# A projection's biases added in place in PSUM by VectorE, in place of bf16 products on TensorE

## The chip, the cores and the metric

The kernel runs on one core of one Trainium2 chip. The metric is the device time of one execution in microseconds (us); the span of the profile is the time from the first to the last instruction of the profiled execution. A core has five engines with a queue each, worked off in order: TensorE (PE; its weight loads are shown as PEld), VectorE (DVE), ScalarE (ACT), GpSimd (POOL) and SyncE (SP), which issues nearly all DMAs here. Engines wait for one another through semaphores. TensorE writes its results into PSUM, and VectorE and ScalarE read them there.

## The reference, cut to what matters

There are 128 graphs of 128 nodes with 64 features, and a dense matrix `adj` for each graph. The first layer is an edge network of 192 hidden units, the second one product with `adj` and a 64x64 matrix.

```python
h = jnp.maximum(_layernorm(x), 0.0)
mask = (adj > 0.0)
xj_proj = h @ W1a                               # W1a, W1b: halves of W1, 64x192 each
diff = h[:, :, None, :] - h[:, None, :, :]
e = relu(xj_proj[:, :, None, :] + diff @ W1b + b1)
hm = einsum('bjkh,bjk->bjh', e, mask)           # sum over the neighbours k of j
x = x + hm @ W2 + deg[..., None] * b2
h = jnp.maximum(_layernorm(x), 0.0)
x = x + einsum('bnm,bmf->bnf', adj, h) @ W.T
```

The sum inside relu splits into one term of node j, `h_j @ (W1a + W1b) + b1`, and one of node k, `-h_k @ W1b`. Both are projections of the nodes, made once for a graph. The biases in question are `b1` in the term of node j, and a bias of 64 columns beside it, made from `b1`, `W2` and `b2`, which is later multiplied by the degree.

## The kernel before

**Staging.** The graphs are worked in 32 groups of 4. A group has 24 jobs. A job fills a tile `g` of PSUM (two banks; a pool of three such tiles) by products on PE that select the projected rows of up to 12 neighbours ("slots") of each of 64 nodes, and then drains it. Jobs of kind 0 are drained by DVE (`hm<-g`, one reduction of 128x768), jobs of kind 1 by ACT (`T<-g`), and POOL adds up their slots (`T<-T`). The table `ORDER` has four jobs of kind 0, two of kind 1, and so on. I number the jobs of a group from 0 to 23; jobs 4, 5, 10, 11, 16, 17, 22 and 23 are of kind 1.

**What is woven in.** After each job's fill the tables `AHEAD`, `OWN` and `BEHIND` call pieces of work for the next group, this one, and the one before. Those around the change are, in order of jobs:

- after job 7: `pre_proj(g, 0)` of the next group, the projection of graphs 0 and 2 of that group;
- after job 8: `post0` (`py` on PE, then `ys<-py` on ACT); after job 10: `post1` (`pty` on PE reads `ys`; then `x1` and its norm on DVE);
- after job 9: `pre_edge_a` (`et<-iov` on ACT); after job 12: `pre_proj(g, 1)`, for graphs 1 and 3, and then `pre_stack`;
- after jobs 14 and 15: `edge_x` (`px` on PE, `X<-px` on ACT); after job 15: `post2` (four `h<-x` on ACT, tile `h2`); after job 16: `post3` (`pga` on PE reads `h2`).

**The projection.** `pre_proj` takes one of the three tiles of the pool of `g`, as `pp`: two banks, one for each graph of the pair. For each graph one fp32 product fills 448 columns: 192 of node k, 192 of node j, and 64 of the second layer's share. A second, bf16, product of a matrix of ones (`oneb`) and `biasp` adds the biases to columns 192 to 447. `biasp` holds them as three bf16 parts in three rows, made at the start in `weights_c` with the help of `id64`. Then ACT copies the first 384 columns to bf16 (`ca<-pp`), and makes `z<-pp` (four instructions) and `e<-pp` (two) from `pp`; DVE subtracts (`rest<-pp,ca`); ACT rounds the rest (`ca<-rest`), and POOL makes the third bf16 part (`ca<-rest,ca`). `pre_stack` copies the three parts by 12 DMAs on SP's queue into `k3` (`k<-ca` in the profile), from which the next group's jobs 0 and 1 read first. Ahead of them stand 12 DMAs `S<-S` on the same queue.

**What sets the order.** The products keep the order of the program on PE. On the other engines the order is fixed in the program only for the first group; after that, in each queue, a scheduler places the instructions when the kernel is built. It also chooses which of the three tiles of PSUM each `g` and `pp` takes. All engines' instructions go through one helper, so most of them carry the line of that helper (L198; L181 and L184 for products and transposes); the groups of the profile are told apart by their tiles.

Of the kernel before, what the change touches and what calls it, by code (L numbers as in the profile page):

```python
# [8 lines left out]
F32 = mybir.dt.float32  # L9
BF16 = mybir.dt.bfloat16  # L10
I32 = mybir.dt.int32
AF = mybir.ActivationFunctionType
ALU = mybir.AluOpType
# [137 lines left out]
def kernel(  # L151
# [28 lines left out]
    def mm(*args, **kw):  # L180
        return tc.keep_in_program_order(nc.tensor.matmul(*args, **kw))  # L181
# [21 lines left out]
    vec, act, pool, sp = (Engine(e) for e in (nc.vector, nc.scalar, nc.gpsimd, nc.sync))  # L203

    B, N, F = x.shape
    H = W1.shape[1]
    O = W2.shape[1]
    P = 128
# [19 lines left out]
    with ExitStack() as main:  # L228
        const = main.enter_context(tc.tile_pool(name="const", bufs=1))
        loads = main.enter_context(tc.tile_pool(name="loads", bufs=2))  # L230
        grp = main.enter_context(tc.tile_pool(name="grp", bufs=2))
        one = main.enter_context(tc.tile_pool(name="one", bufs=1))
# [4 lines left out]
        def gtile(name):  # L237
            return ps_g.tile([P, 2, 512], F32, tag="g", name=name)
# [14 lines left out]
        ident = const.tile([P, P], F32, tag="ident", name="ident")  # L253
        make_identity(nc, ident)

        id64 = const.tile([P, 4], F32, tag="id64", name="id64")
        vec.tensor_tensor(id64, ident[:, 0:4], ident[:, F : F + 4], ALU.add)
        ones = const.tile([P, P], F32, tag="ones", name="ones")
        pool.memset(ones, 1.0)
        oneb = const.tile([P, P], BF16, tag="oneb", name="oneb")  # L260
# [11 lines left out]
        for q in range(Q):  # L272
            s = slice(q * QN, (q + 1) * QN)
# [43 lines left out]
        bias = const.tile([P, H + O], F32, tag="bias", name="bias")  # L317
        wp = const.tile([P, 2 * H + O], F32, tag="wp", name="wp")
        wab = wp[:, H : 2 * H]
        biasp = const.tile([P, H + O], BF16, tag="biasp", name="biasp")  # L320

        def weight_loads():
            act.dma_start(w2a, W2[0:C0, :])
# [22 lines left out]
        def weights_b():  # L346
            pb = mtile("pb")
            mm(pb[:, 0:O], b1x, w2h, start=True, stop=True)
            vec.tensor_tensor(wab, w1[:, 0], w1[:, 1], ALU.add)
            pw = mtile("pw")  # L350
            tp(pw[:, 0:P], wab[:, 0:C0], ident)
            vec.tensor_tensor(bias[:, H : H + O], pb[:, 0:O], b2s, ALU.add)
            vec.tensor_scalar(wp[:, 0:H], w1[:, 1], -1.0, None, ALU.mult)
            vec.tensor_copy(wT, pw[:, 0:P])
            pc = mtile("pc")
            mm(pc[:, 0:O], wT, w2h, start=True, stop=True)
            return pc

        def weights_c(pc):
            left = bias  # L360
            for i in range(3):
                pt = one.tile([P, H + O], BF16, tag=f"bp{i}", name=f"bp{i}")
                vec.tensor_copy(pt, left)

                if i == 0:
                    vec.tensor_scalar(biasp, pt, id64[:, i : i + 1], None, ALU.mult)
                    vec.tensor_copy(wp[:, 2 * H : 2 * H + O], pc[:, 0:O])
                else:
                    vec.scalar_tensor_tensor(
                        biasp, pt, id64[:, i : i + 1], biasp, ALU.mult, ALU.add  # L370
                    )
                if i < 2:
                    nxt = one.tile([P, H + O], F32, tag=f"br{i}", name=f"br{i}")
                    vec.tensor_tensor(nxt, left, pt, ALU.subtract)
                    left = nxt

        def weights_d():
            pl = mtile("pl")
# [5 lines left out]
        def bc(t, n, axis):  # L384
            shape = list(t.shape)
            shape.insert(axis, n)
            return t.unsqueeze(axis).to_broadcast(shape)
# [150 lines left out]
        def pre_proj(g, r):  # L538

            d = groups[g]  # L540
            if r == 0:

                d["ca"] = grp.tile([P, 3, 2, G, H], BF16, tag="ca", name=f"ca{g}")

                d["z"] = grp.tile([P, G, H], F32, tag="z", name=f"z{g}")
                d["e"] = grp.tile([P, G, O], F32, tag="e", name=f"e{g}", bufs=3)
            pp = gtile(f"pp{g}_{r}")
            for p in range(2):
                s = slice(p * F, (p + 1) * F)
                mm(  # L550
                    pp[:, p, 0 : 2 * H + O], d["hT"][s, r], wp[s, :],
                    start=True, stop=False, skip_group_check=True,
                )
            for p in range(2):
                s = slice(p * F, (p + 1) * F)
                mm(
                    pp[:, p, H : 2 * H + O], oneb[s, :], biasp[s, :],
                    start=False, stop=True, skip_group_check=True,
                )
            x = pp[:, :, 0 : 2 * H].rearrange("n p (t u) -> n p t u", t=2)  # L560
            parts = [
                d["ca"][:, i].rearrange("n t (p r) u -> n r p t u", p=2)[:, r] for i in range(3)
            ]
            act.activation(parts[0], x, AF.Copy)
            rest = tmp.tile([P, 2, 2, H], F32, tag="rest", name=f"rest{g}_{r}")

            def zs():
                for p in range(2):
                    b = 2 * p + r
                    for us, f in ((slice(0, C0), AF.Abs), (slice(C0, H), AF.Relu)):  # L570
                        act.activation(
                            d["z"][:, b, us], x[:, p, 1, us], f, scale=d["ns"][:, b : b + 1]
                        )


            def es():
                for p in range(2):
                    b = 2 * p + r
                    act.activation(
                        d["e"][:, b], pp[:, p, 2 * H : 2 * H + O], AF.Copy,  # L580
                        scale=d["dn"][:, 0, b : b + 1],
                    )

            def second():
                act.activation(parts[1], rest, AF.Copy)

            def third(engine):
                for t in range(2):
                    engine.tensor_tensor(
                        parts[2][:, :, t], rest[:, :, t], parts[1][:, :, t], ALU.subtract  # L590
                    )

            def add_x():
                pool.tensor_tensor(d["e"], d["e"], d["x"], ALU.add)

            if g == 0:
                vec.tensor_tensor(rest, x, parts[0], ALU.subtract)
                return zs, es, second, third, add_x
            zs()
            es()  # L600
            vec.tensor_tensor(rest, x, parts[0], ALU.subtract)
            second()
            third(pool)
            if r == 1:
                add_x()
# [205 lines left out]
        class Job:  # L811
# [76 lines left out]
            5: (pre_count,),  # L888
            6: (lambda g: pre_slots(g, 4, D),),
            7: (lambda g: pre_proj(g, 0),),  # L890
            9: (pre_edge_a,),
            12: (lambda g: pre_proj(g, 1), pre_stack,),
            19: (pre_edge_b,),
            20: (pre_place,),
# [51 lines left out]
        pc = weights_b()  # L946
        load(1)
        weight_loads2()
        pre_hT(0)
        first_ranks(0, 0)  # L950
        weights_c(pc)
        constants()
        pre_rank(0)
        pre_count(0)
        steps = [pre_proj(0, 0), pre_proj(0, 1)]
        for (zs, es, second, third, add_x), engine in zip(steps, (pool, vec)):
            if engine is vec:
# [69 lines left out]
```

## Time and profile before

| | |
|---|---|
| time, median of 3 runs (lowest to highest) | 1011.81 us (1011.59 to 1017.17) |
| span of the profiled execution | 1013.2 us, 1.4 us above the median |
| PE, PEld busy | 963.8 us (95%), 721.6 us (71%) |
| DVE, ACT, POOL busy | 799.7 us (79%), 704.1 us (69%), 765.9 us (76%) |
| fp32 products `pp<-wp,hT` | 256 rows, 68.7 us busy |
| `hm<-g` on DVE | 512, 472.1 us busy, 948 ns each |
| HBM | 13.01 MB read, 4.19 MB written, 17 GB/s over the span |

The profile was taken of one execution; its page gives the span and no other time of that execution, and the single stages below are read from it. In its rows, out<-in names the tiles, and the number after a group is the busy time; "idle before" is the time that the engine stood still ahead of it, with what released it. Products overlap on PE and their ends are modelled, so a busy share of 95% doesn't say that PE has no time to spare. HBM's traffic is small against the time; the DMAs that matter are those between tiles of SBUF.

### The profile page before, as it was taken

The page shows a single profiled execution, that of the slowest core. Times are in us where ns is not written, and L with a number is a line of the kernel's source. Part 1 is how long each engine was busy: PE and PEld are TensorE (multiplying, and loading weights), DVE is VectorE, ACT ScalarE, POOL GpSimd, SP SyncE. Part 2 cuts the span into 40 slices and gives each one's busy share as a digit, 9 for nine tenths or more (in the row PEclk, how much of TensorE's full clock was granted, in tenths as well). Part 3 has the DMA queues.
Part 4 walks back from the last instruction along what each step waited for, and adds up shares of the span by engine and source line. Part 5 has one row for each costly group of instructions (what it writes and reads, how often), then busy time and mean ns, then how long its engine had stood idle before and what let it go on. Part 6 is the DMA issues. An engine that isn't in the chain of part 4 may idle for free.

```text
span 1013.2 us, 27270 instructions
## 1 busy us (share of the span) xinstructions
PE 963.8 (95%) x10314; PEld 721.6 (71%) x10314; DVE 799.7 (79%) x1769; ACT 704.1 (69%) x1732; POOL 765.9 (76%) x1134
## 2 busy tenths in 40 slices
PE   3899999999999999999999999999999999999996
PEld 2577777777777777777777777777767777777774
DVE  7767888777888877788877788877787877788863
ACT  5557876677777667777667787667786667787652
POOL 3278777787877777877778877777877778877783
PEclk9599999999999999999999999999999999999998
DMA  3526655556755556766555766545765555765420
GB/s 83 133 68 162 147 135 130 123 124 154 161 136 134 122 120 140 163 136 138 126 123 129 162 144 136 131 112 128 162 140 133 127 120 132 162 147 119 110 67 14
DMA packets 88296, 129.94 MB, mean 128 GB/s; under 512 B 47200, under 2 KB 63968, under 8 KB 88160
## 3 DMA queue, kind: packets, MB, share of 16 engines
q1 hardware_dynamic: 87584, 127.98, 55.2%
q8 instruction: 83, 1.36, 0.5%
q14 instruction: 53, 0.43, 0.1%
q10 hardware_dynamic: 576, 0.16, 0.1%
HBM read 13.01 MB, written 4.19 MB: 17 GB/s over the span
## 4 chain that ended last, share of the span: by engine, by line
PE 45%; DVE 25%; ACT 14%; DMA 5%; POOL 4%; issue 3%; SPq 2%; DVEq 1%; POOLq 0%; ACTq 0%
PE g L181 24%; DVE hm L198 9%; PE pe L181 8%; DVE S L198 8%; DMA k<-ca 4%; ACT ca L198 3%; PE px L181 3%; DVE u L198 3%; ACT et L198 3%; POOL T L198 3%; SPq L198 2%; PE pp L181 2%; PE py L181 2%; ACT h L198 2%; ACT T L198 2%
## 5 line engine op out<-in xcount | busy, mean ns | idle before, releaser
L198 POOL TENSOR_TENSOR T<-T 128x192 f32<-128x192 f32 (+2 forms) x768 | 543.6, 714 | 139.0 <-ACT T L198 99.1
L181 PEld LDWEIGHTS <-k 96*128 96x128 bf16 (+1 forms) x6144 | 412.4, 104 | 208.5 <-issue 87.4
L198 DVE TENSOR_REDUCE hm<-g 128x64 f32<-128x768 f32 x512 | 472.1, 948 | 110.4 <-PE g L181 108.6
L181 PE MATMUL g<-S,k 96*128 96x384 bf16 (+1 forms) x2048 | 392.1, 333 | 29.2 <-DMA k<-ca 14.3
L181 PE MATMUL g<-id,k 96*128 96x192 bf16 (+1 forms) x4096 | 384.1, 248 | 0.0
L198 ACT ACTIVATE T<-g 128x768 f32<-128x768 f32 x256 | 209.8, 821 | 48.5 <-PE g L181 48.5
L198 POOL TENSOR_TENSOR ca<-rest,ca 128x384 bf16<-128x384 f32 x126 | 114.0, 924 | 82.3 <-ACT ca L198 72.0
L198 ACT ACTIVATE ca<-pp 128x768 bf16<-128x768 f32 x64 | 51.3, 802 | 63.9 <-PE pp L181 63.9
L198 DVE TENSOR_TENSOR S<-qs,rks 128x1024 bf16<-128x1024 bf16 x93 | 86.9, 962 | 0.1
L198 ACT ACTIVATE hT<-ph 128x256 f32<-128x256 f32 x32 | 12.3, 383 | 104.0 <-PE ph L184 104.0
L181 PE MATMUL pe<-RT,X 128*64 128x128 f32 (+1 forms) x512 | 74.9, 285 | 0.0
L181 PE MATMUL pe<-mident,z 128*64 128x128 f32 (+1 forms) x512 | 68.8, 274 | 0.0
L181 PE MATMUL pp<-wp,hT 64*128 64x448 f32 x256 | 68.7, 614 | 0.0
L198 ACT ACTIVATE z<-pp,ns 128x128 f32<-128x128 f32 (+1 forms) x256 | 65.7, 347 | 0.0
L198 ACT ACTIVATE ca<-rest 128x768 bf16<-128x768 f32 x64 | 55.2, 863 | 11.6 <-DVE rest L198 11.6
L198 DVE TENSOR_TENSOR rest<-pp,ca 128x768 f32<-128x768 f32 x64 | 60.7, 948 | 3.2 <-ACT ca L198 3.1
L198 DVE TENSOR_SCALAR maskT<-adjT 128x512 bf16<-128x512 f32 x32 | 17.2, 538 | 52.7 <-PE pe L181 52.7
L198 ACT ACTIVATE et<-et,half 128x128 f32<-128x128 f32 x128 | 56.8, 449 | 0.0
L181 PEld LDWEIGHTS pe<-mident,z 128*64 128x64 f32 (+1 forms) x512 | 53.8, 164 | 0.0
L181 PEld LDWEIGHTS pe<-RT,X 128*64 128x64 f32 (+1 forms) x512 | 52.8, 164 | 0.1
L181 PE MATMUL px<-ca,S 128*128 128x192 bf16 x384 | 52.7, 246 | 0.0
L181 PE MATMUL px<-ca,R 128*128 128x192 bf16 x384 | 52.6, 246 | 0.0
(128 smaller groups left out, 1263.1 us busy)
## 6 DMA issues: line engine op xcount, KB each, us to landing
S<-S SPq DMA_DIRECT2D x372, 192.0 KB, 4.0
k<-ca SPq DMA_DIRECT2D x384, 96.0 KB, 2.2
adj<-in_adj_dram SPq DMA_DIRECT2D x32, 256.0 KB, 3.0
x<-in_x_dram SPq DMA_DIRECT2D x32, 128.0 KB, 2.7
out_dram<-ot SPq DMA_DIRECT2D x32, 128.0 KB, 2.2
w<-in_L_gnn_W_dram SPq DMA_DIRECT2D x2, 96.0 KB, 5.1
bias<-in_L_gnn_b_dram ACTq DMA_DIRECT2D x1, 96.0 KB, 4.6
w2a<-in_L_gnn_W_dram ACTq DMA_DIRECT2D x1, 32.0 KB, 2.2
```

Source lines behind the costliest of these rows:

```text
L181: return tc.keep_in_program_order(nc.tensor.matmul(*args, **kw))
L198: ins = f(*args, **kw)
```

## The change

The two bf16 products of each `pre_proj` are taken out. In their place one VectorE operation adds the biases to both graphs' columns 192 to 447 in place in PSUM. It reads `pp` (128 partitions, 2 x 256 fp32) and the fp32 tile `bias`, repeated for the two graphs. The ACT copies and everything else that reads `pp` now come after that operation. `weights_c` keeps one copy of what it did, since the bf16 parts of the biases are not needed, and `id64` goes.

```diff
-        id64 = const.tile([P, 4], F32, tag="id64", name="id64")
-        vec.tensor_tensor(id64, ident[:, 0:4], ident[:, F : F + 4], ALU.add)
...
-        biasp = const.tile([P, H + O], BF16, tag="biasp", name="biasp")
...
         def weights_c(pc):
-            left = bias
-            for i in range(3):
-                pt = one.tile([P, H + O], BF16, tag=f"bp{i}", name=f"bp{i}")
-                vec.tensor_copy(pt, left)
-
-                if i == 0:
-                    vec.tensor_scalar(biasp, pt, id64[:, i : i + 1], None, ALU.mult)
-                    vec.tensor_copy(wp[:, 2 * H : 2 * H + O], pc[:, 0:O])
-                else:
-                    vec.scalar_tensor_tensor(
-                        biasp, pt, id64[:, i : i + 1], biasp, ALU.mult, ALU.add
-                    )
-                if i < 2:
-                    nxt = one.tile([P, H + O], F32, tag=f"br{i}", name=f"br{i}")
-                    vec.tensor_tensor(nxt, left, pt, ALU.subtract)
-                    left = nxt
+            vec.tensor_copy(wp[:, 2 * H : 2 * H + O], pc[:, 0:O])
...
                 mm(
                     pp[:, p, 0 : 2 * H + O], d["hT"][s, r], wp[s, :],
-                    start=True, stop=False, skip_group_check=True,
-                )
-            for p in range(2):
-                s = slice(p * F, (p + 1) * F)
-                mm(
-                    pp[:, p, H : 2 * H + O], oneb[s, :], biasp[s, :],
-                    start=False, stop=True, skip_group_check=True,
-                )
+                    start=True, stop=True, skip_group_check=True,
+                )
+            biased = pp[:, :, H : 2 * H + O]
+            vec.tensor_tensor(biased, biased, bc(bias, 2, 1), ALU.add)
```

## The prediction

> **What bounds the kernel now.** I began with the page, its busy shares and the chain that ended last.
>
> ```profile
> PE 963.8 (95%) x10314; PEld 721.6 (71%) x10314; DVE 799.7 (79%) x1769; ACT 704.1 (69%) x1732; POOL 765.9 (76%) x1134
> PE 45%; DVE 25%; ACT 14%; DMA 5%; POOL 4%; issue 3%; SPq 2%; DVEq 1%; POOLq 0%; ACTq 0%
> ```
>
> PE leads both lines, but the chain changes engines: no engine alone is the end. So I took the sums of the waits, and then one group from the middle of the timeline.
>
> ```profile
> DVE hm L198 <- PE g L181: 108.6, 113, 2.5
> ACT ca L198 <- PE pp L181: 63.9, 34, 3.5
> PE g L181 <- DMA k<-ca: 14.3, 17, 7.2
> PE g L181 <- DVE hm L198: 12.7, 31, 0.5
> ```
>
> Once in nearly every group ACT stands ready for `ca<-pp` before PE has made `pp` (63.9 us in 34 waits), and PE's next job waits a little for a reduction (31 times 0.4 us).
>
> ```profile
> 466.23 1.02 PE L181 MATMUL pp<-wp,hT 64*128 64x448 f32 x4
> ...
> 466.73 0.94 DVE L198 TENSOR_REDUCE hm<-g 128x64 f32<-128x768 f32 x1
> ...
> 467.08 0.28 PE L181 MATMUL pp<-biasp,oneb 64*128 64x256 bf16 x2
> 467.40 0.81 ACT L198 ACTIVATE ca<-pp 128x768 bf16<-128x768 f32 x1 [1.87 <-PE pp L181]
> 467.73 0.48 PE L181 MATMUL g<-S,k 96*128 96x384 bf16 x2 [0.37 <-DVE hm L198]
> 467.80 1.81 DVE L198 TENSOR_REDUCE hm<-g 128x64 f32<-128x768 f32 x2
> 469.00 0.55 ACT L198 ACTIVATE e<-pp,dn 128x64 f32<-128x64 f32 x2
> 469.79 0.38 ACT L198 ACTIVATE ys<-py 128x256 f32<-128x256 f32 x1 [0.25 <-PE py L181]
> 471.15 0.44 PE L184 MATMUL pty<-ident,ys 128*128 128x128 f32 x2
> 473.91 0.28 PE L181 MATMUL pp<-biasp,oneb 64*128 64x256 bf16 x2
> 474.17 0.48 PE L181 MATMUL g<-S,k 96*128 96x384 bf16 x2
> 474.37 0.79 ACT L198 ACTIVATE ca<-pp 128x768 bf16<-128x768 f32 x1
> 477.42 0.81 ACT L198 ACTIVATE h<-x,mrb,rsb 128x64 f32<-128x64 f32 x2
> 478.89 0.61 PE L181 MATMUL pga<-adjT,h 128*64 128x128 f32 x8
> ```
>
> A row holds start, duration, engine and tiles; the bracket is the idle time before it. The next group's `pp` starts at 496.27, so a group takes 30.04 us. After the first `ca<-pp` (467.40) ACT goes from row to row almost without a gap until R at 481.98: in the 15.6 us to 483.0 it is idle for 0.9. PE gets to `pga` at 478.89, and the last of the four `h` that it reads ended at 477.42 + 0.81 = 478.23. ACT is thus only about 0.7 us ahead of PE there. A second limit stands at the end of the group, on SP's queue: 12 DMAs `S<-S` from 466.76, 12 `k<-ca` behind them from 476.79, and the jobs of the next group just catch the last ones.
>
> ```profile
> 485.62 0.33 PE L181 MATMUL g<-S,k 96*128 96x384 bf16 x1
> 486.12 0.32 PE L181 MATMUL g<-S,k 96*128 96x384 bf16 x1 [0.17 <-DMA k<-ca]
> ```
>
> Two such products elsewhere follow each other by 0.16 us, here by 0.50, and in job 1 0.15 more is lost: 0.5 us in a group.
>
> **The change part by part.** *Removed from PE:* a pair of bias products in each of 64 calls. The pair costs 474.17 - 473.91 = 0.26 us of PE's time; 64 x 0.26 = 16.6 us if nothing else stood in the way. At r = 0 job 8 starts at 467.73 because of the reduction of job 6, with or without the pair. At r = 1 the 0.26 us are lost again in the wait for `h` below. I count both at nothing; were PE bare of those waits they would be the 16.6 us of the first rival.
>
> *Added on DVE:* 64 adds of 128x512 fp32. No row of before writes PSUM from DVE. The nearest is `S<-pgq`, 512 elements from PSUM with an operand in SBUF, 691 ns; below stands `x<-pty,e` with 256 elements, 425 ns, and above `rest<-pp,ca` with 768, 946 ns. I take 0.69. That is 44 us on DVE, and its 799.7 become some 842, which still fits into the span. So what counts is where the add stands. In the order in which the changed kernel's instructions stand, DVE does the reductions of jobs 6 and 7, then the add, then those of jobs 8 and 9, and only then `rest`. Behind the waiting add are queued those reductions, which release tiles to jobs 10 and 11.
>
> *The first add (r = 0).* The two reductions from 467.80 step by 0.87 us, so the add runs from 468.67 to 469.36, though `pp` is ready at 467.25. With about 0.05 us for the semaphore, `ca<-pp` starts at 469.41 and not at 467.40: 2.01 us late, of which 0.69 is the add and the rest its place behind job 7. `ca`, `z`, `e` take 2.15 us (467.40 to 469.55), so `e` ends at 471.56 and `ys`, next on ACT, at 471.94. PE needs `ys` for `pty`: 472.0 in place of 471.15, 0.85 us. PE fills no other job meanwhile, because its order is fixed.
>
> *The second add (r = 1).* `pp` comes 0.85 us later and ends at 473.90 + 1.02 = 474.92. DVE has then reduced job 12 (to about 474.9), and the add ends at 475.66. ACT isn't there yet. From 471.94 it has T 0.71, `ca<-rest` 0.75, four `et<-iov` 1.17, T 0.69, sqrt 0.18, and two `et` at 0.30 (one of them moved ahead of `ca`): 476.04. The second add is hidden behind ACT by 0.4 us.
>
> *ACT up to `pga`.* The order is changed here too: after `ca<-pp` 0.69, `z` 0.89, `e` 0.39 come X 0.42, three `h` at 0.33, `ca<-rest` 0.73, X 0.42 and the last `h` 0.48, 5.01 us in all, to 481.05. Two rows, `ca<-rest` and the second X, now stand ahead of the fourth `h`. The fourth product of `pga` started at 478.89 + 3/4 x 0.44 = 479.22, and now at 481.10: PE is 1.88 us late, the 0.85 of `pty` included. Nothing later in the group has that much to spare, since PE's order after `pga` runs on without waits.
>
> *SP's queue.* The DMAs keep their order. `S<-S` still leave at 466.76. The first four `k<-ca` wait for `ca<-pp` (to 476.83, where SP was free at 476.79), the next four for `ca<-rest` (480.31; they were issued from 480.00). So the last land about 0.35 us later, while PE comes 1.88 us later: the 0.5 us of waiting for `k` go away. Tiles of PSUM: job 11 no longer takes the tile of the first `pp`; the second `pp` does, and `rest` (to 472.57) is done by then.
>
> *At the start.* Eight small DVE operations between 9.18 and 12.54 go, and let `pp` begin about 0.7 us earlier; two adds and their order give it back, and `k<-ca` leaves about 0.3 us later.
>
> *Sum.* 1.88 - 0.50 = 1.38 us for each of 31 groups is 42.8 us, with the start 43.1: 1013.2 + 43.1 = 1056.3 us of span, and 1.4 less on the scale of the median: **1055 us**.
>
> **A rule against the trace.** The Trainium skill (Perfetto Trace Analysis, Identifying the Most-Contended Engine) says that matmul busy time is no good measure, that weight loads are to be read in its place, and that DVE's and ACT's occupancy may be taken as it is. By it DVE at 79% is ahead of PEld at 71%, and the change loads the fuller engine; yet with some 842 us DVE would still fit, and occupancy alone would leave the time at 1012. The timeline's gaps decide, not the shares.
>
> **The rivals.**
> - *PE is the bound and DVE has room* (faster). For it: 95%, and DVE idles 108.6 us ahead of reductions. Against it: ACT with 0.9 us of idle time in 15.6, and the fixed order. It needs the add to end within 0.3 us of `pp`, and the 16.6 us to survive: 1012 - 17 = 995 us. Chance 0.06.
> - *Hidden* (within 1%): the 0.7 us of slack ahead of `pga`, the 0.5 us of `k` and the removed products cover a delay of some 1.2 us in a group. The delay at `ca<-pp` would have to be about 1 us, half of what I have. 1012 us, 0.04.
> - *SP's queue stays the limit.* If `k<-ca` slips as far as PE, the 0.5 us are not returned: 31 x 0.5 = 15.5 us more, 1070 us. Against it: the first four are bound to ACT by only 0.04 us. 0.17.
> - *The second add is seen too*, by a slower write to PSUM or late reductions behind it that hold job 15: 0.69 x 31 = 21 us more, 1076 us. 0.08.
> - My forecast 0.65.
>
> **How the numbers follow.** The price of the add enters once a group: 425 ns gives 8 us less, 946 ns 8 us more. If the 0.37 us wait of job 8 for job 6 vanishes in the looser group, 11.5 us less. Low: 1055 - 8 - 12, rounded to 1034. High: 1055 + 8 + 15.5, some 1078. Below 1034 I leave 0.10, above 1078 0.08. About 1% is what a measurement of this kernel can tell from no change; faster 0.06, same 0.04, slower 0.90.
>
> **What would show it.** Right: 64 DVE rows `pp<-pp,bias` near 0.69 us; ACT's idle time ahead of `ca<-pp` at about 31 x 3.9 = 120 us and ended by DVE; PE idle ahead of `pty` (31 x 0.8 = 25 us) and ahead of `pga` (31 x 1 = 31 us), both ended by ACT; PE's wait for `k<-ca` nearly down to the first group's 7.2 us; a group of 31.4 us. Wrong: a group under 30.5 us, or waits for `k<-ca` that grow, or jobs that wait for DVE's reductions in place of ACT.

## The result, and the profile after

The changed kernel took 1048.54 us (median of 4 runs, 1048.07 to 1050.67), the kernel before 1011.7 us beside it (1009.57 to 1017.17). The ratio is 1.035, with a 95% interval of 1.031 to 1.039: slower by 36.8 us. The profiled execution has a span of 1046.4 us, against 1013.2 us before. Where a run of either kernel lists both, the time lies about 1.7 us above the span; so the execution of the kernel before that was profiled would have an estimated 1014.9 us, 3.2 us above its median. That is why the spans differ by 33.2 us and the medians by 36.8.

The page's busy line and the chain that ended last:

```profile
PE 956.1 (91%) x10186; PEld 723.7 (69%) x10186; DVE 849.6 (81%) x1824; ACT 699.3 (67%) x1732; POOL 766.8 (73%) x1134
PE 37%; ACT 29%; DVE 22%; DMA 8%; issue 3%; POOL 1%; DVEq 0%; POOLq 0%; ACTq 0%
```

PE has 128 products fewer and only 7.7 us less to do; DVE has 49.9 us more. On the chain ACT's share rises from 14% to 29%, and that of DVE, which got the new work, falls from 25% to 22% (these shares are rough: the 8% of DMA is `S<-S`, a wrong releaser, as the waits show). The sums of the waits (us, times, longest) say where ACT comes in:

```profile
ACT ca L198 <- DMA S<-S: 116.5, 30, 4.0
PE pga L181 <- ACT h L198: 27.1, 31, 2.7
PE pty L184 <- ACT ys L198: 19.6, 31, 0.6
PE g L181 <- DVE hm L198: 16.2, 32, 0.6
PE g L181 <- DMA k<-ca: 9.1, 1, 9.1
```

PE waits for ACT at two places in every group, `pty` and `pga`. Neither was there before, apart from the first group. Of the 17 waits for `k<-ca` one is left. The first line has to be read with care: it names a DMA, but in every group the wait ends 33 to 34 ns after the end of the add (median add 2.466 to 3.148 us after the start of `pp`, `ca<-pp` at 3.182). What ACT waits for is VectorE.

One group of the timeline, rows of PE, DVE and ACT in order of start:

```profile
478.15 1.02 PE L181 MATMUL pp<-wp,hT 64*128 64x448 f32 x4
479.75 0.94 DVE L198 TENSOR_REDUCE hm<-g 128x64 f32<-128x768 f32 x1
480.61 0.68 DVE L198 TENSOR_TENSOR pp<-pp,bias 128x512 f32<-128x512 f32 x1
481.33 0.81 ACT L198 ACTIVATE ca<-pp 128x768 bf16<-128x768 f32 x1 [3.88 <-DMA S<-S]
483.32 0.43 ACT L198 ACTIVATE ys<-py 128x256 f32<-128x256 f32 x1
483.80 0.44 PE L184 MATMUL pty<-ident,ys 128*128 128x128 f32 x2 [0.64 <-ACT ys L198]
485.71 1.02 PE L181 MATMUL pp<-wp,hT 64*128 64x448 f32 x4
486.78 0.70 DVE L198 TENSOR_TENSOR pp<-pp,bias 128x512 f32<-128x512 f32 x1
487.87 0.79 ACT L198 ACTIVATE ca<-pp 128x768 bf16<-128x768 f32 x1
491.26 0.88 ACT L198 ACTIVATE ca<-rest 128x768 bf16<-128x768 f32 x1
492.00 0.58 ACT L198 ACTIVATE X<-px 128x256 f32<-128x256 f32 x2
492.42 0.49 ACT L198 ACTIVATE h<-x,mrb,rsb 128x64 f32<-128x64 f32 x1
492.95 0.32 PE L181 MATMUL pga<-adjT,h 128*64 128x128 f32 x1 [0.81 <-ACT h L198]
```

The first `pp` is ready at 479.17. DVE is then still to do job 7's reduction (479.75), and the add runs behind it. So `ca<-pp` starts 3.18 us after `pp` began, where it was 1.17 before. `ys` is late with it, and `pty`. The second add ends at 487.48, and ACT comes to `ca<-pp` only at 487.87: hidden. Then `ca<-rest` and two `X` stand ahead of the last `h`, and PE waits for that `h` with the last products of `pga`. The next `pp` starts at 509.67: the group takes 31.52 us.

Laid over 28 groups (group 2 to 29, medians in us after the start of the first `pp`):

| | before | after | later by |
|---|---|---|---|
| first `ca<-pp` | 1.17 | 3.18 | 2.01 |
| `pty` | 4.94 | 5.65 | 0.71 |
| second `pp` | 6.85 | 7.56 | 0.71 |
| fourth product of `pga` | 13.02 | 14.81 | 1.79 |
| `po` | 15.20 | 17.15 | 1.95 |
| job 1 of the next group | 20.81 | 22.46 | 1.65 |
| `pe` | 21.71 | 23.12 | 1.41 |
| next first `pp` (mean) | 30.20 | 31.54 | 1.34 |

So 31 groups would cost 31 x 1.34 = 41.5 us. The spans differ by 33.2 only, because the start gained: the first `pp` of groups 1, 2 and 3 began at 40.85, 75.09 and 105.52 us before, and at 38.66, 68.04 and 99.67 after. At group 2 the changed kernel is 7.0 us ahead, in these two executions.

### The profile page after: what moved, and what is told of

Its sections match the earlier page's. It is cut to its first block, busy times and chain, and to the rows that moved or that the text cites. A ratio compares the mean times of both kernels' runs of the same rounds, so it can differ in the third digit from the quotient of the medians.

```text
span 1046.4 us, 27132 instructions
## 1 busy us (share of the span) xinstructions
PE 956.1 (91%) x10186; PEld 723.7 (69%) x10186; DVE 849.6 (81%) x1824; ACT 699.3 (67%) x1732; POOL 766.8 (73%) x1134
## 3 DMA queue, kind: packets, MB, share of 16 engines
q8 instruction: 82, 1.34, 0.5%
## 4 chain that ended last, share of the span: by engine, by line
PE 37%; ACT 29%; DVE 22%; DMA 8%; issue 3%; POOL 1%; DVEq 0%; POOLq 0%; ACTq 0%
PE g L181 20%; PE pe L181 8%; DMA S<-S 8%; DVE S L198 7%; ACT ca L198 6%; ACT et L198 6%; ACT z L198 5%; ACT h L198 4%; DVE hm L198 4%; ACT X L198 3%; DVE rest L198 3%; DVE u L198 3%; ACT e L198 2%; ACT T L198 2%; PE po L181 1%
## 5 line engine op out<-in xcount | busy, mean ns | idle before, releaser
L181 PEld LDWEIGHTS <-k 96*128 96x128 bf16 (+1 forms) x6144 | 420.4, 104 | 203.1 <-issue 88.8
L181 PE MATMUL g<-id,k 96*128 96x192 bf16 (+1 forms) x4096 | 388.5, 247 | 0.0
L181 PE MATMUL pp<-wp,hT 64*128 64x448 f32 x256 | 66.6, 599 | 0.0
L181 PE MATMUL pga<-adjT,h 128*64 128x128 f32 x256 | 33.5, 284 | 27.1 <-ACT h L198 27.1
```

## Experiments

Theory: the loss is a matter of order on ACT and DVE. The add makes `ca<-pp` late, ACT passes it on to `ys` and `h`, and PE waits for these. Rivals: VectorE is too full for 64 more operations; or the removed products were worth something that was lost on the way; or SP's queue (`k<-ca`) is what really counts.

### One add alone

The add for one r, the bias products for the other (and `biasp` kept):

```diff
+            by_add = r == 1            # second kernel: r == 0
...
+            if by_add:
+                vec.tensor_tensor(biased, biased, bc(bias, 2, 1), ALU.add)
+            else:
+                (bias products as before)
```

Only r = 1. Expected: 

> The add for the second pair of graphs (r = 1) alone; the first pair keeps its bf16 products, and the start keeps its eight operations. My theory (the loss is how late ACT comes to the fourth h that pga reads): the first ca is on time, pty waits for nothing, and the last h ends at about 479.8 on the clock of the group shown of before, where PE came to that product at 479.22. So PE is 0.6 to 0.9 us late in a group and gets the 0.5 us of k back: a group of 30.2 to 30.6 us and 1012 to 1024 us, with PE idle ahead of pga and not ahead of pty. Rival (each add costs its time on DVE, so one of two is half the loss): 1030 us.

Measured 1025.18 us, ratio 1.011 (1.008 to 1.015), just above the range; the group is 30.63 us. The second add is not free by itself: with the first `ca<-pp` in time, the second starts 8.76 in place of 8.16 us after the first `pp`, behind the add, and the fourth product of `pga` is 0.84 us late. In the changed kernel it was hidden only because the first add had made ACT late already.

Only r = 0. Expected: 

> The add for the first pair (r = 0) alone. In its built order ACT has two et, the second rounding and both X ahead of all four h, so they end about 0.6 us later than with both adds. My theory: slower than the full change, a group of about 32.0 us, 1055 to 1078 us, with pty waiting about 0.7 us for ys and pga 2 us or more for h. Rival (a price for each add): half the loss, 1030 us. Rival (only the delay of the first ca counts, whatever stands on ACT): as the full change, 1048 us.

Measured 1069.04 us, ratio 1.054 (1.047 to 1.060), 20 us more than with both adds, as the upper part of the expectation had it. One add fewer is slower, and the timeline says why (ACT, then PE; group from 488.48):

```profile
500.55 0.73 ACT L198 ACTIVATE et<-et,half 128x128 f32<-128x128 f32 x2
501.14 0.88 ACT L198 ACTIVATE ca<-rest 128x768 bf16<-128x768 f32 x1
501.87 0.59 ACT L198 ACTIVATE X<-px 128x256 f32<-128x256 f32 x2
502.29 1.47 ACT L198 ACTIVATE h<-x,mrb,rsb 128x64 f32<-128x64 f32 x4
502.84 0.43 PE L181 MATMUL pga<-adjT,h 128*64 128x128 f32 x2 [0.86 <-ACT h L198]
```

The scheduler has put everything ahead of all four `h`. In place of one late `h` there are four, and `pga` waits twice in a group, 0.86 and 0.22 us, which is half of the 2 us expected; the group is 32.16 us. The order on ACT outweighs an add.

### The same work on VectorE, off the path

The kernel before, with one more operation of the same shape on DVE behind `rest`, into a spare tile that nobody reads:

```diff
             vec.tensor_tensor(rest, x, parts[0], ALU.subtract)
+            spare = one.tile([P, 2, H + O], BF16, tag="br0", ...)
+            vec.tensor_tensor(spare, pp[:, :, H : 2 * H + O], bc(bias, 2, 1), ALU.add)
             second()
```

Expected: 

> The kernel before, bf16 products and all, with an add of the same size beside it: it reads the same columns of pp and the bias, writes a spare bf16 tile that nobody reads, and stands behind rest. DVE gets the same 44 us more, and no copy on ACT waits for it. My theory: little, since the add is on nobody's path but the reductions behind it are 0.7 us late: 1011 to 1026 us. Rival (DVE's load is the cost): as the change, 1048 us.

Measured 1019.42 us, ratio 1.003 (1.000 to 1.006), with DVE at 843.2 us. The load by itself is 0.3% of the 3.5%; the rest hangs on the place.

### Moving what stands in the way

In the changed kernel the second rounding of r = 1 (`ca<-rest`) is held behind the four `h`, and the 12 DMAs `k<-ca` are called after it:

```diff
+            15: (pre_round, pre_stack),       # AHEAD: second(), third(), add_x() of r = 1
...
+        tc.keep_in_program_order(normed)       # the four h
+        tc.keep_in_program_order(second())     # ca<-rest behind them
```

Expected: 

> The change, with the second rounding of r = 1 given out behind post2, and held behind the four h on ACT; both adds and the late first ca stay. My theory: the fourth h no longer waits behind ca<-rest and the second X (1.15 us), so pga waits for nothing beyond the 0.7 us that pty lost; but the last eight k<-ca leave some 1 us later, and may bind again. A group of 30.5 to 31.0 us, 1017 to 1034 us. Rival (the adds and the late ca decide, the order of ACT behind them does not): 1048 us.

Measured 1034.32 us, ratio 1.019 (1.013 to 1.025), just above the upper edge of 1034. PE's waits:

```profile
PE pty L184 <- ACT ys L198: 19.6, 31, 0.6
PE g L181 <- DMA k<-ca: 13.1, 12, 8.6
PE pga L181 <- ACT h L198: 2.7, 1, 2.7
```

The wait ahead of `pga` is gone but for the first group, that ahead of `pty` is untouched, and the waits for `k<-ca` return, eleven more. The fourth product of `pga` is 1.07 us earlier than in the changed kernel, the group (30.96) only 0.58 shorter: with those waits nearly half of it goes again.

The other place: products and add of r = 0 stand ahead of job 7's reduction, the add and that reduction kept in order.

```diff
                 job.fill()
+                if t == 7 and 0 < g < NG - 1:
+                    groups[g + 1]["pp"] = pre_sums(g + 1, 0)   # products, then the add
                 job.drain()
```

Expected: 

> The products and the add of r = 0 stand ahead of job 7's reduction on VectorE, so the add no longer waits for that reduction; the add itself and ScalarE's order behind it are as in the changed kernel. If the place in VectorE's queue is the larger part of the delay at r = 0: ca<-pp about 0.9 us earlier, PE's wait ahead of pty (19.6 us in 31) gone, a group near 31.1 in place of 31.53 us, and 1034 to 1044 us. Rival: PE is held only by the late fourth h, which depends on ScalarE's order and not on pty: then 1045 to 1051 us.

Measured 1041.74 us, ratio 1.029 (1.024 to 1.033), inside the range. `ca<-pp` starts 2.31 us after `pp` in place of 3.18, `pty` waits no more, and the group is 31.29 us. Of the 0.71 us at `pty` 0.25 reaches the end of the group: `pga` still waits for the fourth `h` (29.5 us in 31).

Both together. Expected: 

> Both edits together: the add of r = 0 ahead of job 7's reduction, and the second rounding of r = 1 behind the four h on ScalarE. The adds stay, 64 of them, and so does VectorE's load. Theory (the loss is order alone): no wait of PE ahead of pty or pga, the waits for k<-ca back at 13 to 16 us, a group of 30.2 to 30.5 us, and 1006 to 1022 us. Rival (VectorE, with 44 us more, is too full to be hidden): reductions late at some other job, a group over 30.9 us and over 1030 us.

Measured 1028.31 us, ratio 1.014 (1.011 to 1.018); the expectation ended at 1022. Neither `pty` nor `pga` waits in the groups, and yet the group is 30.74 us and not 30.2 to 30.5. The wait that is left, and one place of it in the timeline:

```profile
PE g L181 <- DVE hm L198: 30.5, 61, 0.6
...
505.34 0.95 DVE L198 TENSOR_TENSOR rest<-pp,ca 128x768 f32<-128x768 f32 x1
...
506.79 0.61 DVE L198 BATCH_NORM_STATS2 stb<-x 128x6 f32<-128x64 f32 x4
507.31 0.36 DVE L198 BATCH_NORM_AGGREGATE mvb<-stb 128x2 f32<-128x6 f32 x4
507.59 0.92 DVE L198 TENSOR_REDUCE hm<-g 128x64 f32<-128x768 f32 x1
508.57 0.48 PE L181 MATMUL g<-S,k 96*128 96x384 bf16 x2 [0.48 <-DVE hm L198]
```

Jobs wait for reductions twice in a group, not once. Here DVE has no gap from `rest` on, which the add has pushed back, and job 12's reduction ends only 0.06 us ahead of job 13. PE gets to `px` 2.80 us after the second `pp`; before, 2.43. That is 0.38 of the 0.55 us that the group is longer, and here the rival of the full VectorE is right: with PE in time, DVE has no room in this stretch. The run with the early add alone has the same second wait (61 waits, `px` at 2.80), and the kernels in which PE came here 0.7 us later, the changed one and the one with `h` first, do not (32 and 31 waits, 2.43). Orders not tried may do better.

### What the products had cost

The changed kernel without the adds:

```diff
-            vec.tensor_tensor(biased, biased, bc(bias, 2, 1), ALU.add)
```

Expected: 

> Neither products nor adds: the two biases of the projection are left out of the computation, all else is the changed kernel. It gives what the products cost in the kernel before. Theory (the bias products stood in time that PE waited anyway, and k<-ca through SP's queue is next): a group of 29.9 to 30.2 us, and with the earlier start 998 to 1008 us. Rival (PE bound, the 16.6 us of the products come back in full on top of the earlier start): 985 to 994 us. Second rival (nothing at all is gained): 1009 to 1014 us.

Measured 1009.75 us, ratio 0.996 (0.994 to 0.999). That is in the range of the second rival. The group is 30.25 us, not shorter than before; what is gained is the start (group 2 begins at 66.83 us, before at 75.09, and the clock has a part in that: see below). So the 16.6 us of products are worth nothing in the groups, and a way of adding these biases, in the order that the scheduler gave this kernel, can win some 0.4% at most (0.1 to 0.6). Why the pair at r = 1 costs nothing, two rows of the kernel without biases show:

```profile
467.24 1.02 PE L181 MATMUL pp<-wp,hT 64*128 64x448 f32 x4
468.36 0.48 PE L181 MATMUL g<-S,k 96*128 96x384 bf16 x2
```

The job's first product starts 1.12 us after the start of the fp32 products. With the pair between them, in the kernel before, it was 1.12 us too (473.05 to 474.17): by the rows, the pair (from 473.91) ran in the end of the fp32 products (to 474.07).

### SP's queue

The sum gave back 0.5 us a group for `k<-ca`. To try that term by itself, in the kernel before, `S<-S` was split: four of the six slots in 12 DMAs as soon as they are made, the last two in 12 smaller ones.

```diff
-            if last < D: return
+            if first == 0: ...; return
+            lo = 0 if last < D else first
...
+                        d["S3"][part * QN : (part + 1) * QN, q, lo:last],
+                        d["S"][q * QN : (q + 1) * QN, lo:last],
```

Expected: 

> The kernel before, bias products and all, with S<-S split: the first four of six slots leave in 12 DMAs as soon as they are made, the last two in 12 smaller ones at the old place. It tests the term of the sum that the change gave back, the 0.5 us a group of waiting for k<-ca. Theory (k<-ca stands behind S<-S in SP's queue): k<-ca leaves earlier, until the last four hang on GpSimd's subtraction (480.83 in the group shown), the waits for k<-ca fall to the first group's 7.2 us, a group of 29.7 us, and 996 to 1004 us. Rival (the last k<-ca hang on GpSimd anyway, or 24 smaller DMAs cost the queue as much): 1009 to 1016 us.

Measured 1198.62 us, ratio 1.183 (1.179 to 1.187): outside all that was expected. SP's rows, first before, then split (DVE makes the slots, SP sends, PE waits):

```profile
466.76 9.93 SPq L198 DMA_DIRECT2D S<-S  x12
476.79 8.88 SPq L198 DMA_DIRECT2D k<-ca  x12
```

```profile
505.69 2.09 DVE L198 TENSOR_TENSOR S<-qs,rks 128x1024 bf16<-128x1024 bf16 x2
507.81 16.34 SPq L198 DMA_DIRECT2D S<-S  x24
524.25 7.54 SPq L198 DMA_DIRECT2D k<-ca  x12
531.48 1.12 PE L181 MATMUL g<-S,k 96*128 96x384 bf16 x2 [3.64 <-DMA k<-ca]
```

Two assumptions fell. The slots are made back to back, so the first DMAs leave 0.5 us ahead of `pp` (508.32) in place of 0.5 us behind it, a gain of one microsecond. And a DMA of 128 or 64 KB takes 16.34 / 24 = 0.68 us of the queue, one of 192 KB 9.93 / 12 = 0.83: their number costs, more than their size. `k<-ca` starts 15.9 us after `pp`, before 10.6, and PE waits 3.64 us for it. All three moves together, in the changed kernel. Expected: 

> The adds kept, with all three moves together: the add of r = 0 ahead of job 7's reduction, the second rounding of r = 1 behind the four h, and S<-S split in two. If what is left of e6_early_hfirst's loss is half k<-ca in SP's queue and half job 13's wait for a reduction: a group of 30.4 to 30.6 in place of 30.74 us, and 1018 to 1025 us. Rival (VectorE's reductions alone): 1026 to 1030 us.

Measured 1194.56 us, ratio 1.178 (1.175 to 1.181): the same loss.

The last try left number and size alone, and sent two of the twelve `k<-ca`, of the third part, from ACT's queue:

```diff
+            for q in (1, 3) if g else ():       # in pre_place, near R
+                act.dma_start(d["k3"][2 * QN : 3 * QN, q], d["ca"][q * QN : (q + 1) * QN, 2])
```

Expected: 

> The kernel before, bias products and all, with two of the twelve k<-ca of a group (the third part, quarters 1 and 3) sent from ScalarE's queue around R, the other ten from SP. The bytes and the number of DMAs are the same. If SP's queue is a limit of the kernel before at the end of a group (the 0.5 us that the change gave back): SP is done with k<-ca about 1.3 us earlier, the waits for k<-ca go down to the first group's 7.2 us, a group of 29.7 to 29.9 us, and 998 to 1005 us. Rival (the reductions and PE's own work are the limit and the waits for k<-ca only lie in their shadow): 1009 to 1015 us. Second rival (ScalarE pays for two more issues, some 0.9 us, ahead of R): 1016 to 1035 us.

Measured 1189.38 us, ratio 1.172 (1.169 to 1.175). Again none of the three:

```profile
522.96 1.82 SPq L198 DMA_DIRECT2D k<-ca  x2
527.01 0.51 ACTq L198 DMA_DIRECT2D k<-ca  x1
528.13 0.51 ACTq L198 DMA_DIRECT2D k<-ca  x1
529.14 5.61 SPq L198 DMA_DIRECT2D k<-ca  x8
535.75 0.60 PE L181 MATMUL g<-S,k 96*128 96x384 bf16 x2 [3.85 <-DMA k<-ca]
```

SP stands still from 524.78 to 529.14. In the program the DMAs of both queues take eight semaphores in turn, and each waits for the previous DMA on its semaphore. SP's third `k<-ca` shares one with the first that ACT sends (527.01, and 2.1 us to land by the median of these DMAs), which in turn waits for GpSimd. So the three runs show that a late `k<-ca` reaches PE at the first jobs of a group. Not all of their loss is the wait itself: their traces have 181 to 202 us at half the clock, that of the kernel before 42, and by an estimate (half of the difference, as if PE were the limit there) the clock takes 70 to 80 of the 175 to 185 us. That an earlier `k<-ca` would give the kernel before anything, they don't show: nothing tried made it earlier.

### The start

The changed kernel with the small DVE operations of the start kept, their result unused:

```diff
+            (the split of the bias into biasp, and id64, as in the kernel before)
```

Expected: 

> The changed kernel with the nine small VectorE operations at the start (the identity's sum and the split of the bias) kept, their result unused; the loop is that of the changed kernel. The changed kernel's first groups ran about 7 us earlier than the prediction had them. If that comes from the operations that went at the start: 1053 to 1057 us. Rival: it comes from the first groups themselves (the adds in place of products, or a loop that settles sooner): 1047 to 1050 us.

Measured 1051.98 us, ratio 1.038 (1.033 to 1.043): 3.4 us more than the changed kernel, between the two, but the intervals of the two ratios overlap. Group 2 begins at 72.72 us, in the changed kernel at 68.04, before at 75.09. The granted clock of TensorE (PEclk, the third number from the end) tells more. In the profiled execution of the kernel before it was at half speed for 23.9 us, until 45.19, and then once more; in the changed kernel for 17.1 us, until 36.07, and from there on it was full. The second fall, in the kernel before:

```profile
45.19:48.60 3.41, 1.93 (x29) 1.52 (x29) 3.04 (x8) 2.16 (x5) 1.10 (x2) 1.00 0.98 225
48.60:55.42 6.82, 6.82 (x37) 3.67 (x32) 1.92 (x2) 5.63 (x17) 6.35 (x12) 0.50 0.43 91
```

The traces of the kernels with the add at r = 1 alone, with the work off the path and with two queues have this second fall too. In these four, PE (its busy time is the second number) had waited 1.48 to 2.08 us near 47 us; in the changed kernel 0.62. So this wait was made longer, in the kernel with the start kept, by doing `S2<-pgq` of the first group three times:

```diff
+            for _ in range(1 if g else 3):
                 vec.tensor_tensor(d["S2"], pg..., bc(ioe, G, 1), ALU.is_equal)
```

Expected: 

> The run with the start's operations kept, and S2<-pgq of the first group done three times over instead of once (same result), so that PE waits about 2.0 us for it near 48 us, and not 0.62. In the kernel before and in two variants PE waited 1.48 to 2.08 us there, and the granted clock then fell back to 0.50 to 0.58 for 50 to 55 us. Theory (a stall there, so soon after the clock has risen, takes the clock away again): clock near 0.55 in 50 to 55 us, the second pp about 4 us later than without the stall (near 76.5 us), and 1055 to 1059 us. Rival (the stall costs its own 1.4 us and no more): clock 1.00 from 50 us, 1052.5 to 1054 us.

Measured 1053.64 us, ratio 1.039 (1.036 to 1.042). The time doesn't decide: of the four runs two lie just under the rival's range (1051.96, 1052.46), two at the lower edge of the theory's (1054.83, 1055.02). The trace does. PE waited 2.81 us, and the clock fell, though for 3.41 us only; group 1 took 32.15 us (30.72 without the stall), not 34.24 as before. The kernel without biases has the same wait of 1.48 us as the kernel before, and its clock stayed full. With the stall, then without biases:

```profile
44.34:47.75 3.41, 0.86 (x14) 0.66 (x16) 2.65 (x7) 2.40 (x6) 2.29 (x4) 1.00 1.00 225
47.76:51.16 3.40, 3.40 (x18) 1.36 (x12) 0.96 (x1) 3.40 (x10) 3.24 (x6) 0.50 1.00 208
```

```profile
38.17:41.58 3.41, 2.58 (x32) 2.16 (x31) 3.30 (x6) 3.09 (x10) 0.53 (x1) 1.00 0.99 202
41.58:44.99 3.41, 2.63 (x26) 1.51 (x25) 1.89 (x7) 3.39 (x9) 2.95 (x5) 1.00 0.99 223
```

What sets the two apart is a grid in time. In all 14 traces the clock changes only at steps of 3.41 us, counted from its first change. Of the steps at full clock, the 123 after which it fell had PE standing still for 1.48 us or more, and the 3911 after which it stayed full for 1.29 us or less. In the kernel before, the whole wait of 1.48 us lies in one step; without biases 41.58 cuts it, and the two steps have 0.83 and 0.78.

Where the grid lies against the kernel differs from execution to execution, so the second fall of the kernel before is in part chance. In 58 further executions of it the mean clock goes from 0.978 to 0.990 (0.980 in the profiled one), and the 16 at 0.982 or less have a median of 1017.3 us, the 18 at 0.988 or more 1010.9; which of them had the second fall, no trace shows. The changed kernel's wait of 0.62 us is too short for it anywhere. When the clock first rises is loose as well: with one and the same start, at 46.34 us in the run with the operations kept and at 37.51 in the one with the stall, and group 1 began at 42.00 and 40.09. So the 3.4 us of the first of these runs are no more than the clock can give or take, and that the work that went is part of the gain isn't shown.

## Why the prediction was right, and where its steps were off

The forecast was 1055 us, 6.5 us above the median, and right in kind and place. Its change was 43.1 us; the medians give 36.8. Part of the closeness is luck. The 1.4 us taken off at the end set the span of one execution against the times of others; by the 1.7 us between span and time, a span of 1056.3 would be a time of 1058.0 us. (The low end of the range adds up to 1035, not 1034.)

- **First add.** `ca<-pp` 2.01 us late was forecast and 2.01 was measured, with the add at 0.68 us, the second one 0.70 (forecast 0.69, from `S<-pgq`), and its place behind job 7's reduction. `pty` was to be 0.85 us late and was 0.71. That the place is the larger part, the early add shows: 0.87 us of the 2.01 went, and the add itself is 0.68.
- **Second add.** Hidden behind ACT by 0.4 us: measured 0.40 (add's end at 9.33, `ca<-pp` at 9.73 us after the first `pp`). The run with this add alone shows that only ACT's delay hid it.
- **`pga`.** Forecast 1.88 us late for its fourth product; measured 1.79. The run with `h` first shows the cause: without the two rows ahead of the fourth `h` 1.07 us of it are gone.
- **`k<-ca`.** Forecast 0.50 us given back; from `po` to `pe`, behind jobs 0 and 1, the delay goes from 1.95 to 1.41, so 0.54, and to the next group's `pp` 0.61. One wait is left, as forecast.
- **Products.** Counted at nothing, and nothing they were. The reason given for r = 1, that 0.26 us are lost again in the wait for `h`, was wrong: with the pair or without it, the next job starts after 1.12 us, so there was nothing to lose.
- **The group.** 1.38 us forecast, 1.34 measured; 31.4 and 31.5 us.
- **The term that was off: the start.** It was put at 0.3 us of loss, since eight small operations on DVE (nine went: DVE has 1824 - 1769 = 64 - 9 more instructions) were set against two adds. Measured at group 2 it is a gain of 7.0 us. The steps were counted in durations of DVE, and the clock was left out: up to group 2 PE ran 30.7 us at half the clock in the kernel before and 17.1 in the changed one, and half of the difference, 6.8 us, is an estimate of what that costs, as if PE were the limit there. The shorter wait (0.62 us) is the change's own and the place of the grid is chance, so another pair of executions can show a smaller gain: on the medians the change is 3.6 us dearer than in the spans. In the spans, the 28 groups from group 2 on lose 37.5 us, the next one 0.8 and the end 1.8; with 7.0 of gain at the start that is 33.1 of the 33.2 measured.

Of the rivals, *PE is the bound* falls with the kernel without biases: all products gone is worth 0.4%. *Hidden* would have needed a delay of 1 us at `ca<-pp`. *SP's queue stays the limit* didn't come in, but its mechanism is real: three kernels were 175 to 185 us slower through it, the clock included. *The second add is seen too* came in nowhere in the changed kernel, and did in the kernel with only that add.

The rule on occupancy that was weighed against the trace would have given 1012. DVE has 849.6 us of work now, it fits, and the time is 1048.54: the gaps decided.

## What to carry to other kernels

Ask of an operation that changes engines where it will stand in the new engine's queue, and who is next on the engine that waits for it: here the 0.68 us cost of the add became 2.01 us at its reader through one reduction ahead of it, and 1.79 us on TensorE through two rows of ScalarE's order. Work taken off a busy engine is worth only what stood on the path: leave it out wholly, once, to see about the most that a replacement can win (the order that the scheduler then gives is part of the answer). Before splitting DMAs or spreading them over queues, count the issues and see which semaphore each will wait on.

## What the runs showed of the hardware

**A wait of TensorE can cost more than itself.** In the run with two queues PE stood still for 3.85 us, and then (columns as above):

```profile
536.00:538.00 2.00, 2.00 (x12) 1.65 (x12) 0.96 (x1) 0.11 (x1) 1.50 (x4) 0.52 0.59 136
538.00:540.00 2.00, 2.00 (x14) 1.80 (x13) 0.83 (x1) 0.48 (x1) 0.00 (x0) 0.63 0.41 122
```

Four products `g<-id` took 0.85 us there, and 0.49 elsewhere in that run. The mean granted clock of that run was 0.916, of the kernel before 0.980. The waits of 0.6 and 0.8 us that the change brought left it at 0.987. The Trainium skill (TensorE: Matmul & The Clock Gate, Part 1: The HAM clock gate) says that the clock halves after an idle window of about 3.4 us; the steps of 3.41 us and the 3.85 us here agree with that, but a step need not be idle throughout: in these traces 1.48 us of it were enough, and 1.29 were not.

**A DMA holds SP's queue for about 0.6 us whatever it carries**: 0.59 us by the median for 96 KB in the kernel before, and 0.59 for 64 and 128 KB in the run with split loads. Only at 192 KB did the size show (0.86, before), with the 16 DMA engines full at 209 GB/s (a busy share of 1.02 from 468 to 470 us before).

**A bf16 pair behind fp32 products was free**: 1.12 us from fp32 product to the next job, with and without it.
